# Products of values moved in front of a query product in a fused two-layer attention kernel

## The chip, the cores and the metric

The kernel runs on one core of a Trainium2 chip. The metric is device time in microseconds (us) of one execution, median over repeated runs. All arithmetic is in 32-bit floats, so that every matrix product is issued as two passes on TensorE: a product listed once in the code shows up as two weight loads and two matmuls in the profile.

## The reference

The input has 16 sequences of 256 tokens with 256 features. Two layers follow each other. The first is a linear recurrence gated by a feed-forward network. The second, where the change lies, is this, cut to what matters:

```
xn = layernorm(x)
q  = xn @ Wq                      # 16 heads, 128 plain + 64 rotated columns
c, k_rope = split(xn @ Wkv_a)     # 64 latent + 64 rotated columns, one for all heads
kv = rmsnorm(c) @ Wkv_b           # keys and values of 16 heads from the latent
scores = q . k * scale, causal mask
attn = softmax(scores) @ v        # per head
s  = attn @ Wo
g  = silu(base(xn) + lora of the two best of 8 experts)
out = x + s * g
```

The kernel folds the key and value weights into Wq and Wo, so that scores are products of a 128-row query (64 latent, 64 rotated) with one 128-row key for all heads, and the product of values is softmax times the 64 latent columns.

## The kernel before

**Units and slots.** The 4096 tokens are cut into 8 chunks of 512 (two sequences). The 16 heads are cut into 4 groups of 4. A unit is one group on one sequence, so there are 64 units, 8 in a chunk (`PER`), and the second layer is a loop over i = 0 to 63, one slot for each unit. `r` is the slot's place in its chunk. Slots with i even are the "second slots" of the change (every second slot); `odd` is the other kind. In the text, slot 26 is the one with i = 26.

**Order.** Each engine's instructions in this layer are recorded through a wrapper that ties every instruction to the one before it on its engine, for TensorE (`pe`), VectorE (`ve`), ScalarE (`ac`), GpSimd (`gp`) and SyncE's DMA queue (`sp`). So each engine runs in exactly the written order, and the wait of one instruction holds up all that stand behind it on that engine. All these calls are recorded at one line of the wrapper, L53.

**A unit's way through the engines.** A unit has 8 blocks of 32 queries by 4 heads. `score_pack(u, 0)`, `(u, 1)` and `(u, 2)` compute the scores of the blocks with keys of 256 and 224, then of 192, 160 and 128, then of 96, 64 and 32 columns, each pack in one of three rotating PSUM banks (`sc`). In each pack VectorE adds the mask and takes the negative maximum of each block (`nm`), and ScalarE takes the exponentials into `pr` with their sums `sr`. `normalise` takes reciprocals on VectorE and scales `pr` on GpSimd. In the next slot, VectorE transposes the unit's `pr` in three parts: `turn(w, 1)` and `turn(w, 2)` ahead of pack 1's mask, and `turn(w, 0)` behind pack 1's maxima. Then `send(w)` issues four DMAs on the SP queue that write `turned` to a buffer in DRAM (`far`). Another slot later `fetch` reads it back, rearranged, into `pT` (one DMA of 768 KB on the SP queue, which waits until the four have landed). `values(u)` then multiplies `pT` with the 64 latent columns of `row`: 8 products (16 matmuls) with 64 columns of weights each, `av` in PSUM, which ScalarE copies into `attT`.

**When values are computed.** They come in pairs in even slots: slot i computes `values(units[i - 4])` and then `values(units[i - 3])`. (Slot 4 computes one unit, slot 5 one, and the last units are done after the loop.) The second of the pair was fetched in slot i - 1, and its `turn(w, 0)` and `send` were in slot i - 2.

**Queries.** The queries of group n are built one or two slots ahead by four products of 512 columns (`query_mm(n, 0..3)`, PSUM tile `pq`), parts 0, 1, 2 in an odd slot and part 3 in the even slot behind it. The rotated half goes through VectorE (`qmul`), GpSimd (`qrot`) and then, in the even slot, through `query_move(n)`: eight DMAs on the SP queue from `qrot` into the upper half of `qg`. The latent half is copied by ScalarE (`query_lat`, `qg<-pq`).

**The SP queue.** Its order in a pair of slots, i - 2 even and i - 1 odd, is: fetch of unit i - 4, send of unit i - 3, the eight moves of the queries; then fetch of unit i - 3, send of unit i - 2.

The part of an even slot that the change touches, in the order before:

```
score_pack(u, 0)
...                       # turn(w, 1), turn(w, 2), in some slots mid_chunk
query_mm(n, 3); query_lat(n, 3)
score_pack(u, 1)
turn(w, 0); send(w)
query_move(n)
values(units[i - 4]); values(units[i - 3])
score_pack(u, 2)
```

Of the kernel before, what the change touches and what calls it, by code (L numbers as in the profile page):

```python
# [41 lines left out]
def tile_two_layers(ctx: ExitStack, tc: tile.TileContext, d: dict, out: bass.AP):  # L42
# [181 lines left out]
    def m1(name, shape):  # L224
        return place["pool"].tile(shape, F32, tag=place["tag"], name=name)
# [73 lines left out]
    def key_chunk(ch):  # L299
        k = chunks[ch]  # L300
        pk = m1(f"pk_{ch}", [P, CH])
        for j in range(TPC):
            pe.transpose(pk[:, j * P : (j + 1) * P], k.row[:, j, :], ident)
        k.kT = ak.tile([P, CH], F32, tag="kT", name=f"kT_{ch}")
        ac.copy(k.kT, pk)
# [1013 lines left out]
    def gate_end(ch, jp):  # L1319
        k = chunks[ch]  # L1320
        g = k.g2[:, 2 * jp : 2 * jp + 2, :]
        ve.scalar_tensor_tensor(g, g, 1.0, k.h, ALU.add, ALU.mult)
# [31 lines left out]
    def score_pack(u, pi):  # L1354
        k, b, pack = chunks[u.ch], u.b, PACK[pi]
        if pi == 0:
            u.nm = sm1.tile([P, NQ], F32, tag="nm", name=f"nm_{u.n}", bufs=3)
            u.sr = sm1.tile([P, NQ], F32, tag="sr", name=f"sr_{u.n}", bufs=3)
        qg = groups[u.i // 2].qg
        sc = ps_sc.tile([P, CH], F32, tag="sc", name=f"sc_{u.n}_{pi}")  # L1360
        for a, o in pack:
            pe.matmul(
                sc[:, o : o + 32 * (a + 1)], qg[:, b * NQ + a, :, :].rearrange("p h q -> p (h q)"),
                k.kT[:, b * S : b * S + 32 * (a + 1)], start=True, stop=True,
            )
        ends = [o + 32 * (a + 1) for a, o in pack]
        step = ends[1] - ends[0]
        n = len(pack)
        assert ends == [ends[0] + step * z for z in range(n)]
        if ends[0] - 32 + step * n <= CH:  # L1370
            diag = sc[:, ends[0] - 32 : ends[0] - 32 + step * n].rearrange("p (n s) -> p n s", n=n)[:, :, 0:32]
        else:
            diag = sc[:, ends[0] - step : ends[-1]].rearrange("p (n s) -> p n s", n=n)[:, :, step - 32 : step]
        ve.tensor_tensor(diag, diag, bc(kmask, n), ALU.add)
        for a, o in pack:
            ve.tensor_reduce(
                u.nm[:, a : a + 1], sc[:, o : o + 32 * (a + 1)], AX.X, ALU.max, negate=True
            )
        for a, o in pack:
            w = 32 * (a + 1)  # L1380
            ac.activation(
                u.pr[:, OFF[a] : OFF[a] + w], sc[:, o : o + w], AF.Exp,
                bias=u.nm[:, a : a + 1], accum_out=u.sr[:, a : a + 1],
            )

    def normalise(u, packs):
        blocks = [a for pi in packs for a, _ in PACK[pi]]
        lo, hi = min(blocks), max(blocks) + 1
        ve.reciprocal(u.sr[:, lo:hi], u.sr[:, lo:hi])
        for a in blocks:  # L1390
            v = u.pr[:, OFF[a] : OFF[a] + 32 * (a + 1)]
            gp.tensor_scalar(v, v, u.sr[:, a : a + 1], 1.0, ALU.mult, ALU.mult)
# [30 lines left out]
    def fetch(u):  # L1423
        new_pT(u)
        sp.dma_start(u.pT, u.far.rearrange("k s h z q -> (k s) h z q"))
# [16 lines left out]
    def values(u, e=None):  # L1442
        k, b = chunks[u.ch], u.b
        av = m1(f"av_{u.n}", [P, 2, S])
        for p2 in range(2):
            for kb in range(2):
                for hh in range(2):
                    h = 2 * p2 + hh
                    pe.matmul(
                        av[64 * hh : 64 * hh + 64, p2, P * kb : S].rearrange(  # L1450
                            "p (z s) -> p z s", s=P
                        ),
                        k.row[:, 2 * b + kb, 0:KVL],
                        u.pT[:, h, 2:3, :] if kb else u.pT[:, h, 0:2, :],
                        start=(kb == 0), stop=(kb == 1),
                    )
        if b == 0:
            k.attT.append(a2.tile([P, 2, CH], F32, tag="attT", name=f"attT_{u.n}", bufs=6))
        (e or ac.copy)(k.attT[u.g][:, :, b * S : (b + 1) * S], av)
# [83 lines left out]
    def fast_begin(ch, r):  # L1543

        k = chunks[ch]
        if r == 4:
            fast_sum(ch, (1, 1), (0, 1), (1, 1), ALU.add)
            fast_sum(ch, (0, 1), (0, 0), (0, 1), ALU.subtract)
        elif r == 5:
            fast_sum(ch, (0, 0), (1, 1), (0, 0), ALU.subtract)  # L1550
            fast_out(ch, 0, k.c00, (0,))
        elif r == 6:
            fast_sum(ch, (1, 0), (1, 0), (0, 0), ALU.subtract)
            k.c1 = a2.tile([P, 2, D], F32, tag="h", name=f"c1_{ch}", bufs=1)
            gp.tensor_tensor(k.c1[:, :, 0:DH], k.v, k.p4, ALU.subtract)
            gp.tensor_tensor(k.c1[:, :, DH:D], k.v, k.p5, ALU.add)
            gp.tensor_tensor(k.u, k.u, k.p5, ALU.add)
        elif r == 7:
            fast_out(ch, 1, k.c1, (0, 1))
            fast_store(ch, 1)  # L1560
        elif r == 0:
            fast_out(ch, 0, k.c01, (1,))
            fast_store(ch, 0)
# [38 lines left out]
    units = [Unit(i) for i in range(LAST)]  # L1602
    for i in range(LAST):
        ch, r = divmod(i, PER)
        odd = i % 2 == 1
        u, w = units[i], units[i - 1] if i else None
        here = w is not None and w.i >= LAST - 2
        n = (i + 3) // 2 if odd else (i + 2) // 2
        n = n if n < len(groups) else None
        more = ch + 1 < NCH  # L1610
        last = ch - 1 if ch == NCH - 1 and r in FINISH else None
        fast = ch - 1 if 0 < ch < NCH - 1 else None

        if 2 <= i:
            fetch(units[i - 2])
        score_pack(u, 0)
        if w:
            normalise(w, (2,))
        if fast is not None and r > 3:
            fast_begin(fast, r)  # L1620
        if ch > 1 and r == 0:
            fast_begin(ch - 2, 0)
        out_weights(i)
        if r == 1:
            gate_end(ch, 0)
        if r == 2:
            gate_end(ch, 1)
            if more and ch:
                norm_end(ch + 1)
        if r == 5 and more:  # L1630
            kv_end(ch + 1)
        if i == LAST - 1:

            finish_mm(last, 3, 0, NPAIR)
            finish_out(last, 3)
            last = None
        if w:
            for z in (1, 2):
                turn_here(w, z) if here else turn(w, z)

        if r == 0:
            mid_chunk(ch)
        if r == 7 and more:
            key_chunk(ch + 1)
        if n is not None:
            query_mm(n, 0 if odd else 3)
            if not odd:
                query_lat(n, 3)
        if i == 5:
            values(units[1])  # L1650
        score_pack(u, 1)

        if odd and n is not None:
            query_mm(n, 1)
            query_mul(n, 0)
        if i == 2:
            query_move(n)
        if w:
            if here:
                turn_here(w, 0)  # L1660
            else:
                turn(w, 0)
                send(w)
        if not odd:
            if n is not None and i != 2:
                query_move(n)
            if i >= 4:
                values(units[i - 4])
            if i > 4:
                values(units[i - 3])  # L1670
        score_pack(u, 2)
        normalise(u, (0, 1))

        if odd and n is not None:
            query_mm(n, 2)
            query_mul(n, 1)
            query_rot(n)
            query_lat(n, 2)
        if r < 2:
            gate_begin(ch, r)  # L1680
        if r == 0 and more and ch:
            norm_begin(ch + 1)
        if r == 2 and more:
            transpose_chunk(ch + 1)
        if r == 4 and more:
            kv_begin(ch + 1)
        if r == 6 and more:
            router_chunk(ch + 1)
        if last is not None:
            j = FINISH.index(r)  # L1690
            finish_mm(last, j, 0, NPAIR)
            finish_out(last, j)
        if fast is not None and r in FINISH:
            fast_end(fast, r)
# [95 lines left out]
```

## Time and profile before

| | |
|---|---|
| median of 3 runs | 921.83 us (920.75 to 923.23) |
| span of the profiled execution, first to last instruction | 919.9 us |
| median of the runs less that span | 1.9 us |
| TensorE busy (matmul) | 905.2 us, 98% of the span |
| TensorE weight loads busy | 695.4 us, 76% |
| VectorE, ScalarE, GpSimd busy | 666.4, 465.8, 570.6 us |
| mean granted TensorE clock | 0.996 |
| second layer's loop, first to last slot's first scores | 271.4 to 887.4 us |

Of the profiled execution the span is what is listed; the runs' times are taken from start to end of the whole execution, so a forecast made against the span has 1.9 us added for what lies around it. A busy share of 98% says that TensorE nearly always has a matmul in flight; as matmuls are pipelined (a 512-column pass starts 0.43 us after the one before it, but lasts 0.59 us), the start-to-start distance of groups is the better measure of what something costs.

### The profile page before, as it was taken

To read this page: it belongs to the slowest core of one execution; us is meant where nothing else is said; L and a number is where in the kernel's file an instruction comes from. 1 tells how busy PE (TensorE), PEld (TensorE's weight loads), DVE (VectorE), ACT (ScalarE), POOL (GpSimd) and SP (SyncE) were. 2 spreads that over 40 slices of the span, in tenths; PEclk is the share of its full clock that TensorE was granted. 3 is DMA by queue.
4 is the path that set the end of the run, shared out by engine and by line. 5 is a ranking of instruction groups with operands and counts; after the bars stand their busy time and mean duration, and the time that the engine had idled before them with its cause. 6 is when DMAs were issued, how large, how long until landed. Compare 5 with 4: busy or idle time off the path is not lost.

```text
span 919.9 us, 17382 instructions
## 1 busy us (share of the span) xinstructions
PE 905.2 (98%) x5426; PEld 695.4 (76%) x5426; DVE 666.4 (72%) x2018; ACT 465.8 (51%) x1529; POOL 570.6 (62%) x885
## 2 busy tenths in 40 slices
PE   8999999999999899999999999999999999999998
PEld 7768898987767567777777777777777777777776
DVE  6876687664688779668967866896786689677562
ACT  3335555654336545645644564564466456446541
POOL 1228697777355537686586767648676764866541
PEclk9999999999999999999999999999999999999999
DMA  9730000000025777777776777777677777767771
GB/s 280 232 115 1 1 2 1 1 2 1 1 32 106 201 203 184 203 186 186 178 210 160 208 194 192 189 178 207 159 209 206 181 190 178 205 160 211 206 224 42
DMA packets 196412, 134.00 MB, mean 146 GB/s; under 512 B 142112, under 2 KB 186976, under 8 KB 196320
## 3 DMA queue, kind: packets, MB, share of 16 engines
q1 hardware_dynamic: 194192, 128.68, 53.3%
q0 software_dynamic: 1152, 3.67, 1.2%
q8 instruction: 44, 0.72, 0.3%
q10 hardware_dynamic: 976, 0.53, 0.2%
q14 instruction: 48, 0.39, 0.1%
HBM read 63.11 MB, written 52.95 MB: 126 GB/s over the span
## 4 chain that ended last, share of the span: by engine, by line
PE 90%; DVE 3%; DMA 2%; SPq 2%; POOL 1%; issue 1%; ACT 0%; POOLq 0%; DVEq 0%; ACTq 0%
PE pq L53 22%; PE sc L53 14%; PE po L53 10%; PE av L53 9%; PE r L53 7%; PE f L53 7%; PE ph L53 5%; PE pf L53 5%; PE pg L53 4%; PE pm L53 2%; SPq L53 2%; PE pkv L53 1%; PE tp L53 1%; DMA qg<-qrot 1%; PE py L53 1%; PE pb L53 1%
## 5 line engine op out<-in xcount | busy, mean ns | idle before, releaser
L53 ACT ACTIVATE pr<-sc,nm 128x256 f32<-128x256 f32 (+7 forms) x512 | 189.7, 381 | 240.3 <-DVE sr L53 152.2
L53 POOL TENSOR_SCALAR pr<-pr,sr 128x256 f32<-128x256 f32 (+7 forms) x512 | 192.1, 394 | 190.0 <-DVE sr L53 184.1
L53 PEld LDWEIGHTS sc<-kT,qg 128*128 128x128 f32 x1024 | 157.6, 191 | 62.3 <-issue 40.3
L53 PE MATMUL sc<-kT,qg 128*128 128x256 f32 (+7 forms) x1024 | 176.1, 306 | 5.7 <-DMA qg<-qrot 4.4
L53 DVE TENSOR_REDUCE nm<-sc 128x1 f32<-128x256 f32 (+7 forms) x512 | 127.5, 301 | 6.6
L53 DVE STREAM_TRANSPOSE turned<-pr 128x512 f32<-128x512 f32 x186 | 123.2, 687 | 9.6 <-POOL pr L53 8.7
L53 PE MATMUL pq<-xnT,wlat 128*128 128x512 f32 x256 | 124.1, 608 | 0.0
L53 PE MATMUL pq<-xnT,wrope 128*128 128x512 f32 x256 | 120.2, 593 | 0.0
L53 ACT ACTIVATION_READ_ACCUMULATOR pr<-sc,nm 128x1 f32 x512 | 104.3, 204 | 0.0
L53 DVE TENSOR_TENSOR sc<-sc,kmask 128x96 f32<-128x96 f32 (+1 forms) x192 | 45.5, 237 | 64.9 <-PE sc L53 63.9
L53 PE MATMUL av<-pT,row 128*64 128x256 f32 (+1 forms) x1024 | 90.9, 329 | 0.5 <-DMA pT<-far 0.5
L53 POOL TENSOR_TENSOR qrot<-qmul,qmul 128x512 f32<-128x512 f32 x64 | 83.0, 1317 | 8.0 <-POOL pr L53 2.9
L53 PEld LDWEIGHTS av<-pT,row 128*64 128x64 f32 x1024 | 64.1, 137 | 24.3 <-issue 1.6
L53 DVE TENSOR_TENSOR qmul<-pq,rot_q 128x512 f32<-128x512 f32 x128 | 80.7, 672 | 0.1
L53 ACT ACTIVATE qg<-pq 64x512 f32<-64x512 f32 x128 | 75.4, 589 | 5.4 <-PE pq L53 4.7
L53 PEld LDWEIGHTS pq<-xnT,wlat 128*128 128x128 f32 x256 | 46.0, 192 | 32.0 <-issue 32.0
L53 PEld LDWEIGHTS pq<-xnT,wrope 128*128 128x128 f32 x256 | 45.7, 191 | 32.4 <-issue 32.1
L53 PEld LDWEIGHTS po<-wout,attT 128*128 128x128 f32 x416 | 58.4, 191 | 9.5 <-issue 4.9
L53 PE MATMUL po<-wout,attT 128*128 128x128 f32 (+1 forms) x416 | 64.5, 308 | 0.0
L53 POOL TENSOR_TENSOR rs<-ve,mhalf 128x4 f32<-128x4 f32 (+1 forms) x17 | 16.8, 986 | 51.3 <-DVE ve L53 37.0
L53 PE MATMUL ph<-xnT,p1T 128*128 128x256 f32 (+1 forms) x128 | 44.3, 503 | 0.8 <-DVE xnT L53 0.8
L53 POOL TENSOR_TENSOR attT<-attT,attT 128x512 f32<-128x512 f32 x36 | 45.0, 1270 | 0.0
(226 smaller groups left out, 1505.0 us busy)
## 6 DMA issues: line engine op xcount, KB each, us to landing
far<-turned SPq DMA_DIRECT2D x248, 192.0 KB, 4.3
pT<-far SPq DMA_DIRECT2D x62, 768.0 KB, 5.0
qg<-qrot SPq DMA_DIRECT2D x256, 64.0 KB, 2.3
x<-in_x_dram SPq DMA_DIRECT2D x7, 512.0 KB, 9.3
out_dram<-x POOLq DMA_DIRECT2D x12, 256.0 KB, 4.9
wqn_wo<-in_wq_nopeT_dram SPq DMA_DIRECT2D x4, 512.0 KB, 4.9
wqn_wo<-in_Wo_dram SPq DMA_DIRECT2D x4, 512.0 KB, 6.1
p2T<-in_proj2T_dram SPq DMA_DIRECT2D x2, 512.0 KB, 7.2
```

Source lines behind the costliest of these rows:

```text
L53: r = getattr(self.engine, name)(*args, **kw)
```

## The change

The two calls of `values` in an even slot move from behind `turn(w, 0)`, `send` and `query_move`, ahead of pack 2, to a place in front of `query_mm(n, 3)`, behind pack 0. The same instructions are issued. On TensorE the 32 matmuls of the pair move ahead of the query product (4 matmuls of 512 columns) and of pack 1 (6 matmuls); pack 2 now follows pack 1 directly. On ScalarE the two copies `attT<-av` move ahead of `query_lat(n, 3)` and of pack 1's exponentials. VectorE, GpSimd and the SP queue keep their order. In slot 62 there is no query product left, and the pair then stands in front of pack 1.

```diff
@@ -1642,6 +1642,10 @@
             mid_chunk(ch)
         if r == 7 and more:
             key_chunk(ch + 1)
+        if not odd and i >= 4:
+            values(units[i - 4])
+            if i > 4:
+                values(units[i - 3])
         if n is not None:
             query_mm(n, 0 if odd else 3)
             if not odd:
@@ -1664,10 +1668,6 @@
         if not odd:
             if n is not None and i != 2:
                 query_move(n)
-            if i >= 4:
-                values(units[i - 4])
-            if i > 4:
-                values(units[i - 3])
         score_pack(u, 2)
         normalise(u, (0, 1))
```

## Prediction, made before the result was known

> **What bounds the kernel now.** I read the page first, for the engine that sets the end.
>
> ```profile
> PE 905.2 (98%) x5426; PEld 695.4 (76%) x5426; DVE 666.4 (72%) x2018; ACT 465.8 (51%) x1529; POOL 570.6 (62%) x885
> ...
> PE 90%; DVE 3%; DMA 2%; SPq 2%; POOL 1%; issue 1%; ACT 0%; POOLq 0%; DVEq 0%; ACTq 0%
> ```
>
> TensorE is busy 98%, and the chain that ended last runs 90% through it. So a move on TensorE pays by what it saves between matmuls, and costs what it makes TensorE wait. Next, the timeline of TensorE from the end of slot 25 (odd) through slot 26 (even); columns are start, duration, engine, line, operation, tiles, count.
>
> ```profile
> 518.25 0.75 PE L53 MATMUL sc<-kT,qg 128*128 128x96 f32 x6
> 518.83 1.96 PE L53 MATMUL pq<-xnT,wlat 128*128 128x512 f32 x4
> ...
> 523.22 0.97 PE L53 MATMUL sc<-kT,qg 128*128 128x256 f32 x4
> 524.03 1.88 PE L53 MATMUL pq<-xnT,wlat 128*128 128x512 f32 x4
> 525.75 0.98 PE L53 MATMUL sc<-kT,qg 128*128 128x192 f32 x6
> 526.66 2.82 PE L53 MATMUL av<-pT,row 128*64 128x256 f32 x32
> 529.41 0.85 PE L53 MATMUL sc<-kT,qg 128*128 128x96 f32 x6
> 530.10 1.07 PE L53 MATMUL tp<-ident,xn 128*128 128x128 f32 x8
> ```
>
> No row has idle time: in the middle of the layer TensorE waits for nobody. Start to start, pack 0 takes 0.81 us, the query product 1.72, pack 1 0.91 ahead of values (0.81 without them: 515.71 to 516.53 in slot 25), the pair of values 2.75, pack 2 0.69. The second unit of the pair starts 1.35 us behind the first, at 528.01.
>
> Then the SP queue, which brings the operand `pT` of that second unit, over the same slots:
>
> ```profile
> 510.77 2.71 SPq L53 DMA_DIRECT2D far<-turned  x4
> 513.59 6.70 SPq L53 DMA_DIRECT2D qg<-qrot  x8
> 520.39 0.56 SPq L53 DMA_DIRECT2D pT<-far  x1
> 521.45 2.43 SPq L53 DMA_DIRECT2D far<-turned  x4
> 527.69 0.34 SPq L53 DMA_DIRECT2D pT<-far  x1
> ```
>
> The view of the tile `pT` says how long a fetch takes from issue to landing:
>
> ```profile
> DMA to landing us min/median/max: 4.2/5.0/5.9
> ```
>
> The unit that slot 26 computes second was turned and sent in slot 24 (510.77). Its fetch stands behind eight query moves that hold the queue 6.70 us, is issued at 520.39 and lands at 525.59. Its values start at 528.01: slack 2.42 us. The first unit of the pair was fetched a slot earlier and has some 10 us to spare.
>
> Last, VectorE in slot 24, where this chain starts:
>
> ```profile
> 508.10 0.23 DVE L53 TENSOR_TENSOR sc<-sc,kmask 128x96 f32<-128x96 f32 x1
> 508.37 0.79 DVE L53 TENSOR_REDUCE nm<-sc 128x1 f32<-128x192 f32 x3
> 510.03 0.71 DVE L53 STREAM_TRANSPOSE turned<-pr 128x512 f32<-128x512 f32 x1 [0.88 <-POOL pr L53]
> ```
>
> These are pack 1's mask and maxima, and behind them in strict order the last turn, which ends at 510.74; the send starts 0.03 later.
>
> **Part 1: the boundaries on TensorE.** 30 even slots are touched (4 to 62), nothing is added or removed. Pack 2 takes 0.69 us behind values and 0.58 behind a query product (518.25 to 518.83), 0.11 more, because its first weight load can't start before the 64-column values have drained: the load in the trace starts 0.20 us after the start of the last 128-column values matmul, which alone would take 0.11. In front of the query product that first load is just as exposed; only the later ones hide, and they hid before. The entry into values keeps its 0.10 us too, behind pack 0 instead of pack 1. So the cost is between -0.11 and 0 a slot, -3.3 us and 0 together. I take 0: the values' own first load, in the other direction, is exposed as well (first pair 0.26 us to the next, 0.21 later).
>
> The page "TensorEngine Tiling (Array Packing)" of the Trainium skill, section Tiling Modes, says that a change of tiling mode drains TensorE. The number of changes is the same in both orders, so by it the sum of this part is 0 as well.
>
> **Part 2: the fetch is needed 2.53 us earlier.** The second unit would start at 523.22 + 0.81 + 0.10 + 1.35 = 525.48, against 528.01. Its fetch lands at 525.59, so slot 26 would wait 0.1 us even if nothing else moved; I add 0.1 from landing to the first matmul (0.14 in slot 62, the one slot that waits for a fetch now: landed 885.10, started 885.24).
>
> **Part 3: the same fetch lands later.** Pack 1 of an even slot moves behind values and ends where pack 2 started before. VectorE's mask of pack 1, its three maxima, and the last turn behind them wait for that. From the start of pack 2 in the old trace: 0.31 us to the landing of pack 1's last result, then 0.97 for mask and maxima up to the turn (508.10 to 509.07 in slot 24), 1.28 together. In slot 24: 509.82 + 1.28 = 511.10, against 510.03, so 1.07 later. Send, moves (6.70) and fetch queue behind the turn on SP and all shift with it, and so does the move of the queries that pack 0 of slot 26 needs, which has 1.26 us of slack there (landed 521.96). Wait in slot 26: 2.53 + 1.07 + 0.1 - 2.42 = 1.28 us. A wait in one slot does not add to the next by itself: it delays turn and consumer alike.
>
> The same sum for each even slot, with slack = values' start less landing, and turn delay = start of pack 2 + 1.28 less start of the turn (or of the send, where that waited for an earlier fetch):
>
> - r = 2 (slots 18, 26, 34, 42, 50, 58): slack 1.62, 2.42, 2.70, 2.15, 2.50, 1.99; turn delay 1.0 to 1.1; waits 2.0, 1.3, 1.0, 1.5, 1.2, 1.7: 8.7 us. Slot 10: 1.0 (slack 1.15, its turn waited for GpSimd beyond that).
> - r = 4 (20, 28, 36, 44, 52): slack 1.37 to 1.84, turn delay 0.2 (VectorE was busy with other work until then): 1.5 + 1.2 + 1.1 + 1.0 + 1.0 = 5.8. Slot 12 0.2, as most of its wait is there already (pack 0 waits 1.1 us for the query moves). Slot 60: slack 0.97, delay 1.4: 3.0.
> - r = 6 (14 to 54): slack over 7 us, delay 2.4 to 2.9: none.
> - r = 0 (16 to 56): slack 4.7 to 5.7, delay 2.9: 0.8 + 0.1 + 0.2 + 0.2 + 0.3 = 1.6. Slot 8: 2.4.
> - Slot 62: its query moves and fetch come 1.8 later, and pack 1 now stands behind the late values (0.8): 2.6.
>
> Sum: 8.7 + 1.0 + 5.8 + 0.2 + 3.0 + 1.6 + 2.4 + 2.6 = 25.3 us. With no turn delay anywhere it is about 11. These are the ends for the delay; I take the full one, since pack 1 can't be read before it is computed.
>
> **Part 4: what else moves.** ScalarE's two copies of values (0.59 us each) stand ahead of the query copies and pack 1's exponentials, so these queue behind the second unit's end. Pack 1's exponentials wait for the maxima anyway, until pack 2's old start + 0.6; the query copies end at about + 0.7, so they cost nothing while the maxima cover them, and up to 0.6 us a slot of exponentials if not. Pack 2's masks follow the turn directly; the reciprocals come about 1 us later than at 511.42, and VectorE then waited 1.79 us for `pg` in slot 24, which covers it. The score banks that packs 1 and 2 need were read in the slot before (exponentials over at 522.93 + 0.20, pack 2 at 529.41). `pT` buffers come free earlier, worth nothing.
>
> **The sum.** 919.9 + 25 = 945 of span, + 1.9 around it: 947 us.
>
> **Rivals.**
>
> *The turn is not late* (VectorE's order or another wait covers the delay): only part 2 counts, about 11 us, 933. For it: in r = 4 slots VectorE is the later one already. Against: in r = 0 and 6 TensorE is.
>
> *Waits long enough for the clock.* At the start of the loop, one wait is long:
>
> ```profile
> 321.68 1.05 PE L53 MATMUL sc<-kT,qg 128*128 128x256 f32 x4 [3.47 <-DMA qg<-qrot]
> 322.57 3.35 PE L53 MATMUL pq<-xnT,wlat 128*128 128x512 f32 x4
> ```
>
> Four query matmuls took 3.14 us start to start instead of 1.72; the granted clock was 0.5 for 3.41 us. If the waits of slots 8, 60 and 62 (2.4 to 3.0) do this, each costs up to 1.7 us: 952.
>
> The page "TensorE: Matmul & The Clock Gate", Part 1, has an idle window of about 3.4 us as what halves the clock. By it alone, waits of 1 to 2 us cost nothing more, and this rival is confined to those three slots.
>
> *The softmax of even slots becomes the bound.* Packs 1 and 2 arrive together and pack 1 of the next slot waits for exponentials: 0.5 us in 28 slots, 14 more, 961. Against: the margin is about 1.5 us in slot 27.
>
> *Not slower.* One mechanism at one place: the first load behind values hides under the query product and saves 0.11 us in 30 slots, 918.5. It decides only where the second unit's fetch keeps over 2.6 us of slack; of the 28 slots 8 to 62 only those of r = 6 and most of r = 0 do. The order of instructions shows the move done as written, so a change without effect is no rival.
>
> **Numbers.** Forecast 0.60 (941 to 953), turn not late 0.17, clock 0.12, softmax 0.06, not slower 0.05. The range 932 to 955 takes in the first three. A measurement of this kernel tells about 0.3% (2.8 us) from no change: faster 0.03, same 0.02, slower 0.95.
>
> **What would show it.** Right: waits of about 1 to 2 us, ended by the DMA `pT<-far`, ahead of the second `av` unit in slots with r = 2 and 4 and none at r = 6; the last turn 1 us later in r = 0 slots; pack 2 at 0.58 us; the first query product 0.11 longer. Wrong: no such waits, `av` to `pq` without exposed load, or waits of packs for ScalarE.

## The result, and the profile after

The changed kernel takes 949.95 us (948.09 to 951.96, 4 runs) against 922.53 us: ratio 1.0297, 95% interval 1.0276 to 1.0317. It is slower by 27 us; the forecast was 947. The profiled execution has a span of 949.1 us, 29.2 more than before, on which the readings below rest.

The page first: TensorE's share, and the chain that ended last.

```profile
PE 911.5 (96%) x5426; PEld 695.0 (73%) x5426; DVE 665.8 (70%) x2018; ACT 471.0 (50%) x1529; POOL 571.9 (60%) x885
...
PE 68%; DMA 10%; SPq 8%; DVE 6%; POOL 3%; ACT 2%; issue 2%; ACTq 0%; DVEq 0%; POOLq 0%
```

The matmuls are the same 5426, but the chain runs through TensorE for 68% of the span, not 90%. What came in is DMA, the SP queue (SPq) and VectorE. The view of waits says where TensorE stands still; columns are total us, times, longest.

```profile
PE av L53 <- DMA pT<-far: 17.7, 14, 1.8
PE sc L53 <- DMA qg<-qrot: 3.9, 1, 3.9
PE sc L53 <- DVE sc L53: 3.7, 2, 2.7
PE sc L53 <- issue: 2.8, 3, 2.1
```

The first row is new: before, `av` waited for a fetch once, 0.5 us. The 14 waits stand in slots 10, 18, 26, 34, 42, 50 and 58 (r = 2), in 12, 20, 28, 36, 44 and 60 (r = 4) and in 62; slot 52's, of 0.9 us, is put down to `DVE turned`, though it too ends 0.14 us after its fetch has landed. The wait of 3.9 is slot 6's, which was there (3.5). Now the timeline of TensorE in slot 26.

```profile
534.53 0.97 PE L53 MATMUL sc<-kT,qg 128*128 128x256 f32 x4
535.43 1.52 PE L53 MATMUL av<-pT,row 128*64 128x256 f32 x16
537.98 1.52 PE L53 MATMUL av<-pT,row 128*64 128x256 f32 x16 [1.02 <-DMA pT<-far]
539.43 1.98 PE L53 MATMUL pq<-xnT,wlat 128*128 128x512 f32 x4
541.25 1.57 PE L53 MATMUL sc<-kT,qg 128*128 128x192 f32 x12
542.65 1.07 PE L53 MATMUL tp<-ident,xn 128*128 128x128 f32 x8
```

The two units of values, one row of 32 before, are torn apart by 1.02 us of idle time ended by `pT<-far`. Start to start the pair takes 4.00 us instead of 2.75; the slot takes 9.03 instead of 7.78. All else in the slot sums to what it was: pack 0 0.90, the query product 1.82, packs 1 and 2 together 1.40 (0.91 and 0.69 before).

The same chain on the SP queue and, ahead of it, on VectorE in slot 24 (whose first scores start at 514.40; at 503.19 before):

```profile
520.79 0.34 SPq L53 DMA_DIRECT2D pT<-far  x1
523.16 3.21 SPq L53 DMA_DIRECT2D far<-turned  x4
526.48 5.64 SPq L53 DMA_DIRECT2D qg<-qrot  x8
532.22 0.56 SPq L53 DMA_DIRECT2D pT<-far  x1
```

```profile
521.43 0.27 DVE L53 TENSOR_TENSOR sc<-sc,kmask 128x96 f32<-128x96 f32 x1 [1.89 <-PE sc L53]
521.73 0.79 DVE L53 TENSOR_REDUCE nm<-sc 128x1 f32<-128x192 f32 x3
522.43 0.70 DVE L53 STREAM_TRANSPOSE turned<-pr 128x512 f32<-128x512 f32 x1
```

VectorE's mask now waits 1.89 us for pack 1, and the last turn starts 8.03 us into the slot instead of 6.84. The fetch is issued at 532.22, lands at 537.84, and values start 0.14 later.

Slot by slot (first scores to first scores, worked out from the timeline of TensorE, summed over the 8 places of a chunk), against the prediction's sum:

| place in the chunk | predicted growth, us | measured, us |
|---|---|---|
| r = 2 | 9.7 | 9.6 |
| r = 4 | 9.0 | 11.0 |
| r = 0 | 4.0 | 2.3 |
| r = 6 (all of it in slot 62) | 2.6 | 0.8 |
| odd slots | 0 | 5.9 |
| together | 25.3 | 29.6 |

The loop began 0.4 us earlier than before, hence 29.2 in the span.

In six slots, 14, 22, 30, 38, 46 and 54 (r = 6), the fetch lands in time and the length changes by 0.01 us at most: in this place the pair itself costs nothing.

### The profile page after: what moved, and what is told of

It reads as the page before. It is cut to its first block, busy times and chain, and to the rows that moved or that the text cites. A ratio compares the mean times of both kernels' runs of the same rounds, so it can differ in the third digit from the quotient of the medians.

```text
span 949.1 us, 17344 instructions
## 1 busy us (share of the span) xinstructions
PE 911.5 (96%) x5426; PEld 695.0 (73%) x5426; DVE 665.8 (70%) x2018; ACT 471.0 (50%) x1529; POOL 571.9 (60%) x885
## 4 chain that ended last, share of the span: by engine, by line
PE 68%; DMA 10%; SPq 8%; DVE 6%; POOL 3%; ACT 2%; issue 2%; ACTq 0%; DVEq 0%; POOLq 0%
PE pq L53 14%; PE sc L53 9%; SPq L53 8%; DMA pT<-far 8%; PE av L53 7%; PE po L53 7%; PE r L53 7%; PE f L53 7%; PE ph L53 5%; PE pf L53 4%; POOL pr L53 3%; DVE nm L53 2%; ACT pr L53 2%; PE pg L53 1%; PE pkv L53 1%
## 5 line engine op out<-in xcount | busy, mean ns | idle before, releaser
L53 PEld LDWEIGHTS sc<-kT,qg 128*128 128x128 f32 x1024 | 155.2, 191 | 63.1 <-issue 49.6
L53 PE MATMUL sc<-kT,qg 128*128 128x256 f32 (+7 forms) x1024 | 170.0, 305 | 10.6 <-DMA qg<-qrot 3.9
L53 PE MATMUL av<-pT,row 128*64 128x256 f32 (+1 forms) x1024 | 96.0, 334 | 18.6 <-DMA pT<-far 17.7
L53 PEld LDWEIGHTS av<-pT,row 128*64 128x64 f32 x1024 | 67.2, 138 | 48.7 <-issue 24.0
L53 ACT ACTIVATION_READ_ACCUMULATOR pr<-sc,nm 128x1 f32 x512 | 102.3, 200 | 0.0
L53 PEld LDWEIGHTS pq<-xnT,wlat 128*128 128x128 f32 x256 | 43.9, 190 | 36.6 <-issue 36.0
L53 ACT COPY attT<-av 128x512 f32<-128x512 f32 x62 | 35.8, 589 | 30.6 <-PE av L53 30.6
```

Of the source, the lines that this page charges most:

```text
L53: r = getattr(self.engine, name)(*args, **kw)
```

## Experiments

Two readings stood against each other. The theory: TensorE loses its time waiting for the second unit's fetch, because that is needed earlier and sent later. The rival "place": the pair costs in front of a query product as such, by the change between 128- and 64-column weights or by ScalarE's order. A second question was whether the earlier need and the later turn each carry a share that adds up.

### The turn put ahead of pack 1

```diff
@@ changed kernel, even slots from 4 on
+        turn(w, 0); send(w)
         score_pack(u, 1)
-        turn(w, 0); send(w)
```

> The changed order on TensorE, with the last turn and the send of every even slot put ahead of pack 1's mask on VectorE, so that the turn no longer waits for pack 1 behind the pair. Theory (the loss is the wait of the second unit for its fetch, made of an earlier need and a later turn): in slots r = 0 the turn goes back to where GpSimd's last scaling allows it, 6.9 us after the slot's first scores (8.0 after the change, 6.8 before it); in slots r = 2 to 6.4 (8.7, 7.3); so only the earlier need of 2.53 us is left against slacks of 1.0 to 2.7 us, in part paid by the earlier turn: about 4 us in r = 2, 1 in r = 4, 3 in slots 60 and 62, and the 2.7 us of slot 7 go: 927 us, 924 to 932. Rival 'place' (the pair costs in front of the query product whatever the fetch, by boundaries or ScalarE's order): 947 to 952. Rival 'the shares add up' (11 us for the earlier need, the rest for the later turn): 933 to 936.

Measured: 929.15 us, ratio 1.0082 (1.0064 to 1.0100). The place of the pair is unchanged and three quarters of the loss are gone, so "place" falls. But the split is not as the theory had it: r = 4 fell from 11.0 to 1.9 us, r = 2 only from 9.6 to 7.9, where about 4 was expected, and slots 11 and 61 are 2.5 us shorter than in the kernel before. In slot 26 the pair even takes 4.31 us. The SP queue over slot 24 (first scores 506.31):

```profile
512.72 0.34 SPq L53 DMA_DIRECT2D pT<-far  x1
514.01 2.78 SPq L53 DMA_DIRECT2D far<-turned  x4
516.90 7.33 SPq L53 DMA_DIRECT2D qg<-qrot  x8
524.33 0.56 SPq L53 DMA_DIRECT2D pT<-far  x1
```

The turn is 1.06 us earlier, but the moves hold the queue 7.33 us instead of 5.64. The fetch ahead of them, issued at 512.72, lands only at 520.01, in the middle of the moves; after the change it had landed at 525.10, before the moves began. The fetch of slot 26's second unit is issued 18.02 us after slot 24's first scores, against 17.82 in the change. So here a turn brought back by a microsecond gains nothing, and over the seven slots r = 2 it gains 1.7 us. That the moves are slower because of the fetch in flight is not shown by this alone (see the last section).

### Only the first unit moved

```diff
@@ changed kernel
             values(units[i - 4])
-            if i > 4:
-                values(units[i - 3])
         ...
                 query_move(n)
+            if i > 4:
+                values(units[i - 3])
         score_pack(u, 2)
```

> Only the first unit of the pair (fetched a slot earlier, some 10 us to spare) moves in front of the query product; the second stays in front of pack 2. TensorE now enters and leaves the 64-column products twice in an even slot. Theory: no wait for a fetch, since the second unit starts as late as before, and the turn is at most 1.45 us later where slack covers it; left are one more entry (0.10 us) and one more exit (0.11 us) in 29 slots, 6 us, and about 1 us in slots 7 and 15: 929 us, 926 to 932. If entries and exits were free in this place: 922 to 924. Rival 'place': half of the loss or more, 936 to 952.

Measured: 930.73 us, ratio 1.0094 (1.0080 to 1.0109), and no unit in the loop waits for a fetch; the one wait of `av` (0.3 us) lies behind the scores of slot 63. TensorE in slot 26:

```profile
526.09 0.97 PE L53 MATMUL sc<-kT,qg 128*128 128x256 f32 x4
527.00 1.52 PE L53 MATMUL av<-pT,row 128*64 128x256 f32 x16
528.45 1.98 PE L53 MATMUL pq<-xnT,wlat 128*128 128x512 f32 x4
530.27 0.98 PE L53 MATMUL sc<-kT,qg 128*128 128x192 f32 x6
531.18 1.52 PE L53 MATMUL av<-pT,row 128*64 128x256 f32 x16
532.63 0.85 PE L53 MATMUL sc<-kT,qg 128*128 128x96 f32 x6
```

Start to start: pack 0 0.91 (0.81 without values behind it), a unit alone 1.45 twice (the pair 2.75), the query product 1.82 (1.72). That is 0.10 + 0.15 + 0.10 = 0.35 us more a slot, and every even slot from 14 to 60 is longer by 0.34 to 0.36. Over the 27 even slots from 8 to 60 (slot 10 has 0.28) that is 9.3 us; slot 7 adds 1.1, slots 5, 6, 9, 11, 61 and 62 give 2.5 back, and 7.9 stay in the loop. Of the 2.5, 1.35 are slot 6's: its wait of 3.4 us was followed by half clock in the kernel before and by full clock here. So this kernel loses its time to one more change to 64 columns and back in each slot, and none in the loop to a fetch. I had the price at 0.21; that the total still fell into the theory's range is owed to the 2.5 us that came back.

### Pack 1 ahead of the pair

```diff
@@ kernel before, even slots from 4 on
         score_pack(u, 0)
-        query_mm(n, 3); query_lat(n, 3)
         score_pack(u, 1)
         ...
         values(units[i - 4]); values(units[i - 3])
+        query_mm(n, 3); query_lat(n, 3)
         score_pack(u, 2)
```

> The pair stands in front of the query product, but pack 1 goes ahead of both, so that VectorE's masks and the last turn come no later than before. The second unit is needed 1.72 us earlier than before (2.53 after the change). Theory: waits of 0 to 0.7 us in slots 10, 18, 60 and those with r = 4, about 3 us in all: 925 us, 922 to 928, and no wait at all in most slots. Rival 'place': 945 to 952, since the pair and the query product stand exactly as in the change. Rival 'the shares add up': 1.72 of 2.53 of the 11 us, 929 to 931.

Measured: 925.16 us, ratio 1.0037 (1.0026 to 1.0049), within the theory's range. The pair stands right in front of the query product, as in the change, so "place" falls here too. The waits of `av`:

```profile
PE av L53 <- DMA pT<-far: 1.6, 5, 0.6
```

They are as short as expected, but not where they were expected: they stand in slots 10, 18, 26, 42 and 62, and none in slots r = 4. The total has other parts too: slots 27, 35, 43 and 51 grew by 1.7 us together without a wait for a fetch, and slots 6, 9, 11 and 61 gave 2.8 back.

### Only the turn late

```diff
@@ kernel before, even slots from 4 on
         score_pack(u, 1)
-        turn(w, 0); send(w); query_move(n)
         values(units[i - 4]); values(units[i - 3])
         score_pack(u, 2)
+        turn(w, 0); send(w); query_move(n)
```

> TensorE's order is that of before; only the last turn, the send and the query moves of every even slot from 4 on are issued behind pack 2's mask and maxima, which is where the change puts the turn in time. Theory: the fetch lands 0.4 to 1.2 us later against slacks of 1.0 to 2.7 us, so the second unit hardly waits; about 1 us each in slots 12, 60 and 62 (their query moves are late already), 2 to 3 us in slots 6 to 8: 926 us, 922 to 930. Rival 'the shares add up': the later turn carries its 14 to 16 us by itself: 934 to 939. Rival 'place': 922.

Measured: 930.20 us, ratio 1.0089 (1.0073 to 1.0104), just above the theory's range (922 to 930) and short of the rival's (934 to 939). No unit waits for a fetch, although the turn starts 8.30 us into slot 24: the slack covers it, so the two shares don't add up. TensorE and the SP queue:

```profile
529.24 2.82 PE L53 MATMUL av<-pT,row 128*64 128x256 f32 x32
```

```profile
517.49 5.74 SPq L53 DMA_DIRECT2D qg<-qrot  x8
```

The 8 us went elsewhere, 4.0 of them to slots r = 7 and 2.1 to slots 61 and 62. The eight moves behind the late send land late too, and the next even slot's first scores need them: in slots 8, 16, 24, 32, 40, 48 and 56 pack 0 starts 0.45 to 0.49 us after the last of them has landed. Such a fixed distance says that it waits for them, although the view of waits names other work there (`issue`, `DVE sc`, `ACT pr`).

### Half of the query moves ahead of the send

```diff
@@ changed kernel, even slots from 6 on
+        query_move(n, (0,))      # four of the eight
         turn(w, 0); send(w)
-        query_move(n)
+        query_move(n, (1,))      # the other four
```

> The changed kernel, with four of the eight query moves of each even slot from 6 on issued ahead of the last turn's send instead of behind it. TensorE, VectorE, ScalarE and GpSimd keep the changed order, the turn is as late as in the change; only the SP queue's hold between send and fetch halves, from 5.6 us to about 2.8. Theory (the wait for the second unit's fetch is the loss, and the queue is part of its chain): the fetch is issued some 2 to 2.8 us earlier in slots r = 2 and 1.5 or more in r = 4, so the waits of 1.0 to 1.8 us there go; slots 7 and 15 (3.9 us) and part of slots 59 to 62 stay: 926 us, 921 to 931. Rival 'late turn by itself' (the loss comes through the later masks, maxima and turns, whatever the queue does): 945 to 952. Rival 'transfer' (what the queue gains, the transfers lose by lying on one another: landing of a fetch goes from 4.5 to 6 us or more): 935 to 945.

Measured: 924.44 us, ratio 1.0017 (1.0005 to 1.0029), so 25.5 us of the change's 27 come back, and both rivals fall. TensorE, VectorE, ScalarE and GpSimd run in the changed order, and in slot 24 the turn is as late as in the change (8.01 us in). The SP queue there, and TensorE in slot 26:

```profile
511.30 2.68 SPq L53 DMA_DIRECT2D qg<-qrot  x4
514.02 4.09 SPq L53 DMA_DIRECT2D far<-turned  x4
518.22 3.00 SPq L53 DMA_DIRECT2D qg<-qrot  x4
521.39 0.49 SPq L53 DMA_DIRECT2D pT<-far  x1
```

```profile
524.55 0.97 PE L53 MATMUL sc<-kT,qg 128*128 128x256 f32 x4
525.45 2.82 PE L53 MATMUL av<-pT,row 128*64 128x256 f32 x32
528.20 1.98 PE L53 MATMUL pq<-xnT,wlat 128*128 128x512 f32 x4
```

The fetch lands at 526.13, 21.68 us after slot 24's first scores; in the change 23.44. That is 1.76 us earlier, more than slot 26 had waited, and the pair is whole again. I had expected the issue alone to come 2 to 2.8 us earlier in slots r = 2; it came 0.3 to 1.8 us earlier there (0.87 in slot 26, as the send now holds the queue 4.09 us instead of 3.21), and the rest is a shorter way from issue to landing (4.74 us instead of 5.62). In slots r = 4 the issue came 2.8 to 4.2 us earlier. From slot 26 to 54, r = 2, 4 and 6 all have the length of before to within 0.01 us, and slots 7 and 15 have lost their growth of 2.7 and 1.2. This is the plainest evidence for the cause: only the order of a DMA queue is altered, and the loss goes. Not all of it goes: slots 8, 10, 18 and 56 are still 2.2 us longer together than before, which slots 11 and 61 make up for with 2.5 us, most of it waits that the kernel before had itself.

### Towards a version that beats both

What is left in the kernel before are TensorE's waits in slots 6, 12 and 62. Three versions with the order of TensorE as before tried them. The first splits the moves as above and also issues those of slot 4 ahead of that slot's fetch:

```diff
@@ kernel before with the split
+        if i == 4: query_move(n)
         fetch(units[i - 2])
```

> The kernel before, with the same split of the query moves from slot 6 on, and the moves of slot 4 issued ahead of that slot's fetch, where the queue now stands idle for the landing of a send. TensorE's order is that of before. Theory: only TensorE's waits of before can go: 3.5 us in slot 6 for the query moves and the 1.4 us at half clock behind it, 0.95 in slot 12, part of 1.8 in slot 62; slot 6's second unit may wait 1 to 2 us for its fetch instead: 918 us, 915 to 920. If SP's order matters only through that fetch, and these waits have another cause: 921 to 923.

Measured: 921.57 us, ratio 0.9987 (0.9974 to 0.9999), above the expected range (and within that of the alternative, whose condition is not met, as slot 6's wait did go). Slot 6 no longer waits for queries; its second unit does, for its fetch:

```profile
327.74 2.83 PE L53 MATMUL av<-pT,row 128*64 128x256 f32 x16 [4.03 <-DMA pT<-far]
```

The next kernel takes that unit out of slot 6 into slot 7:

```diff
@@ the version above
-            if i > 4:
+            if i > 6:
                 values(units[i - 3])
         ...
-        if i == 5:
+        if i in (5, 7):
             values(units[i - 4])
```

> The last kernel (before, query moves split from slot 6 on, moves of slot 4 ahead of its fetch), with slot 6 computing only its first unit of values and slot 7 the second, ahead of its pack 1. In the last kernel the 3.6 us won at slot 6's query moves came back as a wait of 4.0 us for that second unit's fetch, and half clock behind it (the pair took 8.31 us instead of 2.75). Theory: the fetch lands at 327.6, before slot 7 needs it; the wait and the slow clock go, one more separate run of values costs 0.35: 917 us, 915 to 919. If the loss only moves on, to the query moves of slot 8: 920 to 922.

Measured: 922.32 us, ratio 1.0003 (0.9990 to 1.0015), again above the theory's range: the loss moves on once more, to the queries of slot 8.

```profile
339.81 1.94 PE L53 MATMUL sc<-kT,qg 128*128 128x256 f32 x4 [4.90 <-DMA qg<-qrot]
```

The last has the split alone, without those two edits:

```diff
@@ kernel before, even slots from 6 on
+        query_move(n, (0,))
         turn(w, 0); send(w)
-        query_move(n)
+        query_move(n, (1,))
```

> The kernel before, with only the split of the query moves from slot 6 on; slots 4 and 6 as before. Theory: slot 6 keeps its wait of 3.5 us and the half clock; only slot 12's 0.95 us, slot 9's 0.2 and some of 59 to 62 go: 920 us, 919 to 921.5.

Measured: 920.34 us, ratio 0.9990 (0.9975 to 1.0004), as expected. Slots 11 and 61, whose lengths hold the waits of the first scores of slots 12 and 62, are shorter by 1.1 and 1.4 us. By the intervals none of the three is more than 0.26% faster than the kernel before; what starves the first slots was moved twice and not removed, and its root was not looked for.

## Why the prediction was right, and where its steps were off

**Part 1, boundaries at 0.** Right: in the six slots r = 6 the change costs 0.01 us at most. Packs 1 and 2 together take 0.20 us less, pack 0 and the query product 0.19 more. I had called 0.11 exposed in front of the query product; the product is 0.10 longer. The rule of the Trainium skill's page "TensorEngine Tiling (Array Packing)", section Tiling Modes, that a change of mode drains TensorE, agrees in sign: one more run of values with a change in and out cost 0.35 us a slot in the kernel with only the first unit moved.

**Parts 2 and 3, the wait for the fetch.** Right in mechanism, and right in place for r = 2, r = 4 and slot 62, where all 14 waits for `pT<-far` stand. For r = 0 the sum had 4.0 us of such waits and the trace shows none over 0.15 us there: slots 16 to 56 grew by 0.8 us together, and slot 8 by 1.5 at half clock (see below). In slot 26 the forecast wait is 1.28 us and the pair grew by 1.25. In slot 12 it was 0.2 us and the slot grew by 2.05: the pair waits 1.82 us for a fetch that took 6.94 us to land. Part 3 was right for a partly wrong reason: it let the queue's hold (6.70 us) and the landing move rigidly with the turn. From slot 24 to the landing the trace has: turn +1.19, send +0.50, moves -1.06, landing +0.42, by sum 1.05 later and measured 1.04. And the turn put ahead of pack 1 left 7.9 of the 9.6 us in r = 2. So the 11 us without a turn delay and the 25 with it are no sum of two causes: the kernel with the pair early and the turn ahead loses 7.4 us, the one with the turn late alone 8.4, and there none at the second unit.

**"r = 6: none".** The step that failed, by 4 us. I followed the late turn of r = 6 slots to the fetch, which has 7 us of slack, and not to the other thing queued behind it, the query moves, which the first scores of the next r = 0 slot need. In the change the first scores of slots 8 and 16 start 0.45 us after the last of these moves has landed (at 342.54 and 429.94), behind idle times of 2.72 and 1.01 us; before, the distance was 0.54 and 2.80. I had counted such a need for slot 26 alone (1.26 us of slack). Slot 7 grew by 2.7 us and slot 15 by 1.2, and the split took both back.

**The total.** That 25.3 came so close to 29.6 is in part luck, as errors of both signs met: the odd slots (5.9 us, at nothing in the sum; slot 61's 0.8 of it is the wait of slot 62's first scores, which the sum had under slot 62) and slot 12 (1.9) were missed and the other slots r = 4 up to 52 were 1.4 too low, while r = 0 and slots 60 and 62 were 4.7 too high.

**Part 4, ScalarE.** Nothing was lost there in the slots r = 6, which have the changed order too, nor, once the moves were split, in the slots r = 2 and 4 from 26 to 54.

**The rivals.** The turn was late. The softmax did not become a bound: apart from slots 7, 15 and 61 all odd slots together grew by 1.1 us. "Not slower" fails on the slack, as said. The clock decides in one slot of the three that I named: the wait ahead of slot 8 was followed by half clock, those in slots 60 (1.47 us) and 62 by full clock. First scores of slot 8, and the granted clock (PEclk, the third number from the right) in that stretch and in slots 12 and 62, behind waits of 1.82 and 2.06 us:

```profile
342.99 1.94 PE L53 MATMUL sc<-kT,qg 128*128 128x256 f32 x4 [2.72 <-DVE sc L53]
```

```profile
342.99:344.80 1.81, 1.81 (x5) 1.45 (x6) 1.52 (x6) 1.45 (x7) 1.35 (x4) 0.50 0.91 356
344.80:346.00 1.20, 1.20 (x7) 0.87 (x7) 1.00 (x5) 0.61 (x2) 1.20 (x3) 0.50 0.99 333
...
389.58:391.00 1.42, 1.42 (x16) 1.11 (x16) 0.00 (x0) 0.00 (x0) 1.42 (x2) 1.00 0.07 25
909.70:911.00 1.30, 1.24 (x6) 0.88 (x8) 0.15 (x1) 0.00 (x0) 1.00 (x3) 1.00 0.46 161
```

An idle time of 2.72 us was followed by half clock (0.50), one of 2.06 us by full clock; slot 8's pack 0 took 1.73 us instead of 0.89. But the length of a gap alone does not decide it. In slot 62 of the kernel with the turn late, 2.46 us were followed by half clock (0.51 from 888.90 to 892.00 us). In slot 6, 3.47 us were followed by half clock in the kernel before, and 3.40 to 3.65 us by full clock in four others; here is the one with only the first unit moved:

```profile
322.38 1.05 PE L53 MATMUL sc<-kT,qg 128*128 128x256 f32 x4 [3.42 <-DMA qg<-qrot]
```

```profile
322.38:325.00 2.62, 2.62 (x21) 1.83 (x22) 1.50 (x5) 0.46 (x2) 2.62 (x3) 1.00 0.75 247
```

The Trainium skill's page "TensorE: Matmul & The Clock Gate", Part 1, gives an idle window of about 3.4 us and says that windows run free of the kernel. Gaps shorter than the window were enough twice here, and gaps as long as it were not enough four times, so the window is no safe bound for a single gap.

## What to carry to other kernels

Before an instruction is moved forward, follow every operand back to its latest issue and compare the slack with the distance moved; 2.5 us forward and an operand about 1 us later, against 1 to 2.7 us of slack, made most of the loss. Where something ahead of a queue becomes late, list everything behind it on that queue, not only the transfer that one is thinking of. And when a wait for a transfer appears, look at the order of its queue first: four of eight short transfers issued in an idle gap gave back 25.5 of 27 us.

## What the runs showed of the hardware that I had not expected

The time that the eight query moves hold the SP queue goes with what else is in flight. In six of the kernels here (the kernel before, the changed one and the first four experiments), between 330 and 865 us of the span, it is 5.8 us in the median (5.5 to 7.2, 102 cases) where the fetch ahead of them had landed when they began, and 7.0 (5.7 to 7.7, 32 cases) where that had 1 to 2.5 us still to go (6.5 in 20 cases with up to 1 us to go, 7.3 in 7 with more than 2.5). The landing of a fetch stretches as well, from medians of 4.4 to 5.2 us to 7.29 us in slot 24 of the kernel with the turn ahead. This is a connection over many slots; no run varied the overlap alone.
